# Graph attention in four layers: the softmax weights transposed in 32x32 blocks by VectorE and ScalarE, layer 3's products issued from a list

## The chip, the core and the metric

The kernel runs on one core of a Trainium2 chip. A core has a matrix engine (TensorE, PE in the profile; its weight loads are PEld), a vector engine (VectorE, DVE), a scalar engine (ScalarE, ACT), GpSimd (POOL) and SyncE (SP), which mainly starts DMA transfers. Each engine works through its own list of instructions in order; semaphores make one wait for another. TensorE reads SBUF and writes PSUM[...]. The metric is the time of one execution on the device in microseconds, the median of several runs.

## What is computed

The input x has 128 graphs of 64 nodes with 512 features, fp32, so 8192 rows; adj has a 64x64 mask for each graph. Four layers run one after the other, each with a residual:

```
h = relu(layernorm(x))
x = x + layer(h, adj)
```

Layers 0 and 2 are attention with 4 heads of 64, layer 1 is attention with 8 heads and a layernorm of its own. In these the weights of a head are

```
sim  = q @ k.T * scale             # 64 x 64 in a graph and head
attn = softmax(where(mask, sim, very negative))
out  = attn @ v                    # then @ Wo + bo
```

Layer 3 forms m = h @ map_w.T, then q and k from m, and sem = h @ gcn_map_w.T. For each of 8 heads the cosine of m's rows is compared with 0.1, the 0/1 result multiplies the softmax of q and k, each row is divided by its sum + 1, and the weights are applied to sem; relu, residual, output. The softmax runs along a row of a 64x64 block, which lies along the free dimension, while the sum over neighbours needs that index on the partitions. So each block of weights has to be transposed between the two. That is what the change is about.

## The kernel before

The rows are worked in 16 steps of 512 (8 graphs, that is four blocks b of 128 rows with two graphs g each), layer by layer. A step of a layer goes through layer norm (scales, normalize), transposes of h (transposes), the projections, the scores and softmax (front), and the weighted sum with the output projection (attention; in layer 3 last).

The projections are large products. Each runs as a scheme of seven half-sized products in place of eight (winograd, lines around 640, with product at L581 for the matmuls): a full one is seven products of eight 128x256 passes. Sums of the operands are made by POOL (L362) or VectorE (L359). The results leave PSUM through ScalarE (L598, L602, L618) and VectorE (L611, L622); three PSUM banks mA, mB and mC are used in turn, and a product can begin in a bank only after ScalarE has read the last one out of it.

The scores of a unit fill two PSUM banks S, 128x1024 values (L870): 16 blocks of 64x64. Layers 0 and 2 have one unit in a step, layers 1 and 3 two, so 96 units in all. On each unit come: a mask (VectorE, L881), the row maximum (L887), subtraction into an SBUF tile E (L889), exp on ScalarE (L892), row sums (L899), a reciprocal (L903) and the division by POOL (L905). In layer 3 the cosine scores (L870 again, of the m tiles), a comparison (L1135), a product (L1144) and more sums come in between.

transposed (L906 to L920) then turns E: eight 128x128 transposes by TensorE against an identity, into two PSUM tiles ptp, each brought to the SBUF tile pt by ScalarE (L919). The weighted sum (L1035, in layer 3 L1175) multiplies pt with v. A 128x128 transpose takes two graphs and two heads at once, so scores puts the two graphs of a block side by side on the free dimension, and two heads one above the other. The mask in SBUF therefore is 128 wide for each block of rows, and holds both graphs on all partitions.

The order of all work is set while the program is built. Every piece of work is a Python generator, a stream, which yields an engine, an assumed duration and a latency before each instruction, or an event to wait for. Order.run takes the stream that can start earliest by these durations, ties by priority (a smaller number first), and emits its instruction. An eviction of PSUM (priority 0) goes ahead of other work on ScalarE and VectorE that would still run when it becomes due (urgent). On the chip the order is fixed; if a stream is late there, what stands behind it on the engine is late too.

Buffers: E has three, pt and S one each, PSUM tiles ptp share two buffers with the transposes of h. Weights go through a ring of four buffers (r_w) in the order of units: q3 takes the buffer of layer 2's w_qk, k3 that of w_vo, which layer 2's last output projection still reads.

The projections of layer 3 were emitted step by step: map, sem, q, k for steps 0 to 13, and for the last two steps map, map, q and k, q and k, sem, sem. norms makes the lengths of m's rows: squares by ScalarE (L809), four small matmuls (mmn, L814), a way through DRAM to spread them over the partitions, and a product by POOL (L850). It waits for the end of layer 2's stores (x_done).

Of the kernel before, what the change touches and what calls it, by code (L numbers as in the profile page):

```python
# [16 lines left out]
N = 64  # L17
# [7 lines left out]
NEG_L3 = -1e10 * 8  # L25

# [201 lines left out]
def gnn_stack(ctx: ExitStack, tc: tile.TileContext, a: dict, out: bass.AP):  # L228
# [26 lines left out]
    r_e = ring("e", 3, [P, 16, N])  # L255
    r_c = ring("c", 1, [P, 2, 512], U8)
    r_pt = ring("pt", 1, [P, 2, 4, P])
    r_adj = ring("adj", 2, [P, TB, P], U8)
    r_n0 = ring("n0", 2, [P, TB, P], U8)
# [74 lines left out]
    for key, _ in units:  # L334
        w_ready[key], w_sums[key] = od.event(), od.event()
    wv_sums = {0: od.event(), 2: od.event()}
# [184 lines left out]
    def transposes(steps):  # L521

        for l, s in steps:
# [20 lines left out]
            if (l, s) == (3, 1):  # L544
                yield x_done[2, NG - 1]
# [149 lines left out]
    st, p_ready, s_ready, p_used, late = {}, {}, {}, {}, []  # L695

    def projections(steps):
        for l, s in steps:
# [37 lines left out]
            else:  # L736
                m_part = yield from map_part(s, z, BT)
                if s < NG - 2:
                    yield from sem_part(s, z, BT, m_part[1])
                    yield from qk_part(s, z, *m_part)  # L740
                else:

                    late.append((s, z, BT, m_part))
        for s, z, BT, m_part in late:
            yield from qk_part(s, z, *m_part)
        for s, z, BT, m_part in late:
            yield from sem_part(s, z, BT, m_part[1])

    def map_part(s, z, BT):
        yield w_ready["map3"]  # L750
        mT, z["m_done"] = yield from r_m.new("mT")
        m_ready = yield from unit(W["map3"], (*BT, w_sums["map3"]), False, Out(quarters(mT), map_b))
        m_sums, z["n_ready"], m_used = od.event(), od.event(), od.event()
        od.spawn(when([m_ready], w_done["map3"] if s == NG - 1 else None), 0)
        od.spawn(sums_after(m_ready, quarters(mT), z, m_sums, s == NG - 1), 1)
        od.spawn(norms(mT, s, m_ready, z["n_ready"], m_used), 3)
        return mT, m_ready, m_sums, m_used

    def qk_part(s, z, mT, m_ready, m_sums, m_used):
        es = []  # L760
        for n in "qk":
            yield w_ready[f"{n}3"]
            yield m_sums
            o, z[f"{n}_done"] = yield from r_qk.new(f"{n}T3")
            es.append((yield from unit(
                W[f"{n}3"], (quarters(mT), z["T"], w_sums[f"{n}3"]), False,
                Out(quarters(o), q_b if n == "q" else k_b))))
            z[n] = o
        z["n"] = mT
        od.spawn(when(es, s_ready[3, s], m_used, z["T_done"]), 0)  # L770

    def sem_part(s, z, BT, m_ready):

        yield w_ready["sem3"]
        V, z["v_done"] = yield from r_v.new("S2")

        def sv(i, k):
            return V[:, 2 * k:2 * k + 2, i * H:(i + 1) * H]
        used = yield from unit(W["sem3"], (*BT, w_sums["sem3"]), True, Out(sv))
        od.spawn(when([m_ready, used], t_done[3, s], h_done[3, s]), 0)  # L780
        rows = od.event()
        od.spawn(add_rows(V, used, rows), 0)
        z["v"] = V
        od.spawn(when([rows], p_ready[3, s]), 0)
# [15 lines left out]

    def norms(mT, s, m_ready, ready, used):

        yield m_ready
        yield x_done[2, NG - 1]
# [12 lines left out]
        yield dve(0.69)  # L817
        nc.vector.tensor_copy(ss, p_)
        pe_.set()
# [4 lines left out]
        se.set()  # L824

# [10 lines left out]
        nr = []  # L836
        for c in range(NC):
# [17 lines left out]
    def scores(lT, rT, npair, blocks):  # L855
        S, e = yield from r_sc.new("sc")
        nch = npair // 2
        nb = len(blocks)
        for b, t in enumerate(blocks):
            for ch in range(nch):  # L860
                j = ch * nb + b
                yield quads(0.235)
                for g in range(2):
                    k = slice(t * P + g * N, t * P + (g + 1) * N)
                    col = slice((2 * j + g) * N, (2 * j + g + 1) * N)
                    for a_ in range(2):
                        for par in range(2):
                            c = 2 * ch + (a_ ^ par)
                            r = slice(par * N, (par + 1) * N)
                            nc.tensor.matmul(S[a_ * N:(a_ + 1) * N, par, col],  # L870
                                             lT[r, c, k], rT[r, c, k], start=True, stop=True)
# [35 lines left out]
    def transposed(E, e):  # L907

        Ev = E.rearrange("p (i g) k -> p i (g k)", g=2)
        o, oe = yield from r_pt.new("pt")  # L910
        for par in range(2):
            pt, pe_ = yield from r_tr.new("ptp")
            for j in range(4):
                yield pe(0.115)
                nc.tensor.transpose(pt[:, j, :], Ev[:, par * 4 + j, :], ident)  # L915
            if par:
                e.set()
            yield act(0.6)
            nc.scalar.copy(o[:, par], pt)  # L919
            pe_.set()  # L920
        return o, oe

    def masks(l, s):

        adj, ae = yield from r_adj.new()
        n = TB * P
        yield load(3.5)
        nc.sync.dma_start(adj.rearrange("p b k -> p (b k)"), a["adj"][:, s * n:(s + 1) * n])
        av = adj.rearrange("p b (g k) -> p (b g) k", k=N)
        n0, ne = yield from r_n0.new()  # L930
        nv = n0.rearrange("p b (g k) -> p (b g) k", k=N)
        if l == 3:
            nz = small.tile([P, TB * 2], U8, tag="nz", name="nz", bufs=1)
# [324 lines left out]
```

## Time and profile before

The kernel takes 2898.45 us, the median of 3 runs (2894.9 to 2902.67). In the profiled execution the granted clock of TensorE was 0.994 on average. Busy time in windows that lie inside one layer each:

| window, us | layer | PE busy | VectorE | ScalarE | POOL |
|---|---|---|---|---|---|
| 30 to 540 | 0 | 509.75 | 356.90 | 267.56 | 338.25 |
| 545 to 1440 | 1 | 893.89 | 500.90 | 400.05 | 379.67 |
| 1450 to 1930 | 2 | 479.59 | 306.41 | 239.31 | 305.49 |
| 1945 to 2750 | 3 | 805.00 | 462.00 | 336.81 | 411.76 |
| 2750 to 2790 | 3 | 34.41 | 22.53 | 12.80 | 10.05 |

In such a table the busy time of each engine is held against the length of the window. The groups of the profile give a line of the code, the engine, what is written and read, the shape and the count, then busy time and mean time of one, then the idle time ahead of them and what ended it. The instructions that the change removes are the L915 group on PE (768 matmuls with a median of 273 ns each by the records, which overlap) and the L919 group on ScalarE (192 of 588 ns).

### The profile page before, as it was taken

To read this page: it belongs to the slowest core of one execution; us is meant where nothing else is said; L and a number is where in the kernel's file an instruction comes from. 1 tells how busy PE (TensorE), PEld (TensorE's weight loads), DVE (VectorE), ACT (ScalarE), POOL (GpSimd) and SP (SyncE) were. 2 spreads that over 40 slices of the span, in tenths; PEclk is the share of its full clock that TensorE was granted. 3 is DMA by queue.
4 is the path that set the end of the run, shared out by engine and by line. 5 is a ranking of instruction groups with operands and counts; after the bars stand their busy time and mean duration, and the time that the engine had idled before them with its cause. 6 is when DMAs were issued, how large, how long until landed. Compare 5 with 4: busy or idle time off the path is not lost.

```text
span 2895.9 us, 64997 instructions
## 1 busy us (share of the span) xinstructions
PE 2853.7 (99%) x27944; PEld 2483.3 (86%) x27944; DVE 1730.6 (60%) x2628; ACT 1315.1 (45%) x2265; POOL 1514.1 (52%) x1158
## 2 busy tenths in 40 slices
PE   8999999999999999999999999999999999999998
PEld 7898988888888888888888898978888888888877
DVE  7766666754565556454557666636665556655446
ACT  4555555444444444433445455544444444344332
POOL 6756566544343433344647656665445544455443
PEclk9999999999999999999999999999999999999999
DMA  4324233221112111112322323323222322232221
GB/s 154 133 90 135 90 121 103 79 74 61 45 46 74 61 46 61 60 61 78 119 90 94 131 90 134 105 88 91 62 63 81 90 69 61 61 83 67 64 62 45
DMA packets 160433, 240.70 MB, mean 83 GB/s; under 512 B 15761, under 2 KB 69009, under 8 KB 160145
## 3 DMA queue, kind: packets, MB, share of 16 engines
q1 hardware_dynamic: 145632, 222.08, 24.4%
q10 hardware_dynamic: 14512, 14.47, 1.5%
q8 instruction: 219, 3.59, 0.5%
q14 instruction: 70, 0.57, 0.1%
HBM read 168.87 MB, written 67.63 MB: 82 GB/s over the span
## 4 chain that ended last, share of the span: by engine, by line
PE 96%; DVE 1%; DMA 1%; POOL 1%; issue 0%; ACT 0%; SPq 0%; DVEq 0%; ACTq 0%; POOLq 0%
PE mA L581 46%; PE mC L581 23%; PE mB L581 11%; PE sc L870 5%; PE ptr L535 3%; PE ptp L915 3%; PE po L1035 2%; PE po L1175 1%; PE ptr L512 1%; PE mmn L814 1%; POOL E L905 0%; DMA w_o<-in_Wo 0%; DMA out<-xres 0%; DMA xin<-in_x 0%; DVE sm L899 0%
## 5 line engine op out<-in xcount | busy, mean ns | idle before, releaser
L981 POOL TENSOR_TENSOR xres<-xres,u 128x512 f32<-128x512 f32 x192 | 247.1, 1294 | 274.7 <-ACT u L976 271.2
L439 DVE BATCH_NORM_STATS2 st<-xin 128x6 f32<-128x512 f32 x320 | 216.8, 678 | 156.0 <-DMA xin<-x 118.1
L960 POOL TENSOR_TENSOR xres<-xres,u 128x512 f32<-128x512 f32 x192 | 267.7, 1415 | 36.0 <-DMA xres<-x 21.8
L446 POOL TENSOR_TENSOR rs<-rs,mhalf 128x2 f32<-128x2 f32 x160 | 115.6, 726 | 276.5 <-DVE rs L444 265.8
L455 ACT ACTIVATE xin<-xin,rs 128x512 f32<-128x512 f32 x320 | 248.9, 810 | 18.4 <-DVE rs L448 17.7
L362 POOL TENSOR_TENSOR t<-hT 128x512 f32<-128x512 f32 x126 | 161.5, 1282 | 114.4 <-ACT hT L517 80.4
L598 ACT COPY v<-mA 128x256 f32<-128x256 f32 (+1 forms) x192 | 91.9, 478 | 282.9 <-PE mA L581 274.4
L581 PE MATMUL mA<-w_vo,t 128*128 128x128 f32 (+1 forms) x1152 | 205.3, 310 | 0.0
L581 PE MATMUL mA<-t,w_q 128*128 128x256 f32 x744 | 190.5, 383 | 0.0
L581 PE MATMUL mA<-t,w_qk 128*128 128x256 f32 x768 | 187.4, 380 | 1.4 <-DVE t L359 1.4
L362 POOL TENSOR_TENSOR t<-hT,t 128x512 f32<-128x512 f32 x126 | 162.7, 1291 | 40.9 <-ACT hT L517 37.3
L905 POOL TENSOR_TENSOR E<-E,sm 128x1024 f32<-128x1024 f32 x64 | 123.4, 1929 | 112.0 <-DVE sm L903 81.4
L581 PEld LDWEIGHTS mA<-w_vo,t 128*128 128x128 f32 x1152 | 168.4, 191 | 12.5 <-ACT u L976 1.1
L899 DVE TENSOR_REDUCE sm<-E 128x16 f32<-128x1024 f32 x128 | 155.3, 1213 | 35.6 <-ACT E L892 34.9
L581 PE MATMUL mA<-t,w_k 128*128 128x256 f32 x744 | 175.9, 379 | 0.0
L581 PEld LDWEIGHTS mA<-t,w_qk 128*128 128x128 f32 x768 | 143.2, 190 | 19.7 <-DVE t L359 1.6
L919 ACT COPY pt<-ptp 128x512 f32<-128x512 f32 x192 | 112.7, 588 | 102.6 <-PE ptp L915 101.4
L581 PEld LDWEIGHTS mA<-t,w_k 128*128 128x128 f32 x744 | 141.2, 190 | 19.1
L976 ACT COPY u<-mA 128x512 f32<-128x512 f32 x144 | 84.4, 586 | 146.7 <-PE mA L581 143.9
L581 PEld LDWEIGHTS mA<-t,w_q 128*128 128x128 f32 x744 | 132.4, 190 | 15.3
L540 ACT COPY hT<-ptr 128x512 f32<-128x512 f32 x192 | 112.7, 588 | 55.0 <-PE ptr L535 55.0
L798 POOL TENSOR_TENSOR v<-v,gcn_row 128x512 f32<-128x512 f32 x64 | 79.2, 1268 | 106.1 <-ACT v L598 106.1
(217 smaller groups left out, 6966.0 us busy)
## 6 DMA issues: line engine op xcount, KB each, us to landing
x<-xres SPq DMA_DIRECT2D x96, 512.0 KB
xin<-x SPq DMA_DIRECT2D x96, 512.0 KB
xres<-x SPq DMA_DIRECT2D x64, 512.0 KB
xres<-in_x SPq DMA_DIRECT2D x32, 512.0 KB
u<-rs SPq DMA_DIRECT2D x128, 128.0 KB
xres<-x SPq DMA_DIRECT2D x64, 256.0 KB
out<-xres SPq DMA_DIRECT2D x64, 256.0 KB
xin<-in_x SPq DMA_DIRECT2D x30, 512.0 KB
```

The costliest lines, as they stand in the source:

```text
L362: nc.gpsimd.tensor_tensor(o, i0, i1, ALU.subtract)
L439: nc.vector.bn_stats(st, v[:, t, :])
L446: nc.gpsimd.tensor_tensor(rs[:, 0, :], rs[:, 1, :], mhalf[:, :2], ALU.pow)
L455: nc.scalar.activation(v[:, t, :], v[:, t, :], func, bias=rs[:, 2, t:t + 1], scale=rs[:, 0, t:t + 1])
L540: nc.scalar.copy(h[:, :, b * P:(b + 1) * P], pt)
L581: nc.tensor.matmul(o, l, r, start=(first and m == 0 and k == 0), stop=(k == KC - 1), skip_group_check=True)
L870: nc.tensor.matmul(S[a_ * N:(a_ + 1) * N, par, col], lT[r, c, k], rT[r, c, k], start=True, stop=True)
L899: nc.vector.tensor_reduce(o, E, AX.X, ALU.add)
L905: nc.gpsimd.tensor_mul(E, E, sm[:, :, None].to_broadcast([P, 16, N]))
L919: nc.scalar.copy(o[:, par], pt)
L960: nc.gpsimd.tensor_add(xr[:, t, :], xr[:, t, :], bo[l])
L981: nc.gpsimd.tensor_add(v, v, both(u))
```

## The change

The transposes leave TensorE. VectorE can transpose each 32x32 block of a tile in place of its own; for a 64x64 block that leaves the two off-diagonal blocks in the wrong places. So ScalarE first copies E to a tile F in eight pieces, each of 32 partitions and 16 x 32 elements, which moves blocks between partitions; then one VectorE instruction transposes all 32x32 blocks of F into pt. E is free after the copies, so it has two buffers; F has one. As blocks are now 64 wide, scores keeps a graph on its own 64 partitions, and masks and cosine masks are half as wide; the host sends half of the mask.

```diff
     def transposed(E, e):
 
-        Ev = E.rearrange("p (i g) k -> p i (g k)", g=2)
+        F, fe = yield from r_f.new("F")
+        for g in range(2):
+            for i in range(2):
+                for k in range(2):
+                    yield act(0.587)
+                    nc.scalar.copy(F[g * N + 32 * k:g * N + 32 * (k + 1), :, 32 * i:32 * (i + 1)],
+                                   E[g * N + 32 * i:g * N + 32 * (i + 1), :, 32 * k:32 * (k + 1)])
+        e.set()
         o, oe = yield from r_pt.new("pt")
-        for par in range(2):
-            pt, pe_ = yield from r_tr.new("ptp")
-            for j in range(4):
-                yield pe(0.115)
-                nc.tensor.transpose(pt[:, j, :], Ev[:, par * 4 + j, :], ident)
-            if par:
-                e.set()
-            yield act(0.6)
-            nc.scalar.copy(o[:, par], pt)
-            pe_.set()
+        yield ("dve", 1.2, 1.0)
+        nc.vector.transpose(o, F)
+        fe.set()
         return o, oe
...
-    r_e = ring("e", 3, [P, 16, N])
+    r_e = ring("e", 2, [P, 16, N])
+    r_f = ring("f", 1, [P, 16, N])
```

The transposes of a unit are no longer called by attention; a stream of their own, turns, takes the units in order and sets pt_ready.

```diff
         for u, blocks in enumerate(units):
-            yield z["e_ready", u]
-            pt, pte = yield from transposed(*z["e", u])
+            yield z["pt_ready", u]
+            pt, pte = z["pt", u]
...
+    def turns(steps):
+
+        for l, s in steps:
+            yield p_used[l, s]
+            z = st[l, s]
+            for u in range(len(units_of(l)[1])):
+                yield z["e_ready", u]
+                z["pt", u] = yield from transposed(*z["e", u])
+                z["pt_ready", u].set()
```

The second part concerns layer 3. Its projections come from a written list; the first two steps are interleaved, so that other products stand between q and k of step 0. What step 1 waits for becomes earlier: o_taken is set when layer 2's last output sums have their buffer.

```diff
+        order = [("map", 0), ("sem", 0), ("q", 0), ("map", 1), ("k", 0), ("sem", 1), ("q", 1), ("k", 1)]
+        for s in range(2, NG - 2):
+            order += [(n, s) for n in ("map", "sem", "q", "k")]
+        order += [(n, s) for n in ("map", "qk", "sem") for s in (NG - 2, NG - 1)]
...
             if (l, s) == (3, 1):
-                yield x_done[2, NG - 1]
+                yield o_taken
...
     def norms(mT, s, m_ready, ready, used):
 
         yield m_ready
-        yield x_done[2, NG - 1]
+        if s == 0:
+            yield o_done
+        elif s < NG - 1:
+            yield lengths[s - 1]
```

Smaller edits of order: residuals of neighbouring steps take their buffers in turn, an output projection waits for the one before it, the copy of the lengths out of PSUM gets priority 0, and the loads of lengths for step 14 wait until step 15 has sent its squares. Outside the 768 transposes, TensorE has the same matmuls as before, in the same shapes.

## The prediction, made before the changed kernel was run

> **What bounds the kernel now.** I read the engines' busy shares first, then the chain that ended last, then TensorE's own waits, then the timeline around the instructions that the change removes.
>
> ```profile
> PE 2853.7 (99%) x27944; PEld 2483.3 (86%) x27944; DVE 1730.6 (60%) x2628; ACT 1315.1 (45%) x2265; POOL 1514.1 (52%) x1158
> ...
> PE 96%; DVE 1%; DMA 1%; POOL 1%; issue 0%; ACT 0%; SPq 0%; DVEq 0%; ACTq 0%; POOLq 0%
> ```
>
> TensorE (PE) is busy 99% of the span and is 96% of the chain. A busy PE need not be one at its peak, so I looked at what it waits for:
>
> ```profile
> PE ptr L535 <- ACT xin L455: 11.2, 1, 11.2
> PE mA L581 <- DMA w_k<-in_k: 4.5, 1, 4.5
> PE mC L581 <- DVE xres L611: 3.7, 1, 3.7
> PE ptp L915 <- POOL E L905: 2.2, 2, 1.9
> ```
>
> The columns are total, times, longest. All of PE's waits come to some 33 us, a third of it the start. Three sit at borders of layers or near the end; in the steady part of a layer PE waits for nobody (from 545 to 1440 us, layer 1, it is busy for 893.89 of 895). So the time is the sum of PE's starts, and an edit is worth what it takes out of that row. What one transpose takes is in the timeline of layer 1:
>
> ```profile
> 601.31 1.03 PE L581 MATMUL mA<-t,w_q 128*128 128x256 f32 x4
> ...
> 602.18 0.60 PE L915 MATMUL ptp<-ident,E 128*128 128x128 f32 x4
> ...
> 602.62 1.89 PE L581 MATMUL mC<-t,w_q 128*128 128x256 f32 x8
> ```
>
> From the start of the four transposes to the start of the next product are 0.44 us, so 0.110 us each, not the 0.273 us of one record: records overlap. Four product passes before them take 602.18 - 601.31 = 0.87 us, 0.217 each, the same as inside a run of products (eight in 1.73 us elsewhere), so switching between the two costs nothing extra.
>
> [...] The record here is 273 ns, but the interval of 110 ns is what counts. [...] The squares of the norms, SBUF to SBUF with 512 elements, agree (619 ns each, started 520 ns apart: four took 2.19 us).
>
> **The change part by part.**
>
> 1. Transposes leave PE. 96 softmax units (16 steps x (1 + 2 + 1 + 2) units) x 8 = 768, the count of the L915 row. 768 x 0.110 = **84.5 us off the path**. The chain's own share, 3% of 2896 rounded, agrees. The products have the same count and shapes, as do scores and weighted sums (32 small matmuls per pair of banks[...]): only which head lies where changes. I take zero for these.
>
> 2. ScalarE. Out: 192 evictions of 588 ns, 112.7 us. In: 96 x 8 = 768 copies of 32 partitions x 512 elements. ScalarE's groups have these rows (busy, mean ns, idle before); the last is the nearest, from SBUF to SBUF:
>
> ```profile
> L455 ACT ACTIVATE xin<-xin,rs 128x512 f32<-128x512 f32 x320 | 248.9, 810 | 18.4 <-DVE rs L448 17.7 <-issue 0.7
> ...
> L919 ACT COPY pt<-ptp 128x512 f32<-128x512 f32 x192 | 112.7, 588 | 102.6 <-PE ptp L915 101.4
> ...
> L809 ACT ACTIVATE u<-m 128x512 f32<-128x512 f32 x64 | 36.5, 621 | 1.0 <-issue 1.0
> ```
>
> I expect 0.52 us apart and 0.61 each; bounds 0.50 and 0.81 (the row of L455, with two pointer operands, should the strided 32-partition form be slow). 768 x 0.52 = 399, so ScalarE goes from 1315 to about 1602, 57% of the new span; upper bound 1315 - 113 + 622 = 1824, 65%. Layer 0 is the densest: 268 us of 510 now (52%), 16 x (8 x 0.52 - 1.18) = 48 more, against 510 - 14 = 496: 64%. Off the path as long as PSUM evictions aren't held up. One copy is a separate instruction, and in the new order evictions stand between the copies (typically one to four copies, an eviction, one to four copies), so an eviction finds at most a few copies ahead of it that were planned there.
>
> 3. VectorE. In: 96 transposes of 128x1024. No row shows one; the nearest is a pass over 1024 fp32 elements:
>
> ```profile
> L899 DVE TENSOR_REDUCE sm<-E 128x16 f32<-128x1024 f32 x128 | 155.3, 1213 | 35.6 <-ACT E L892 34.9
> ```
>
> I take its 1.21 us[...]. 96 x 1.21 = 116. Out: masks on half the columns, as a block's mask is now 64 wide: 64 passes of 0.5 to 1.8 us (28.3 + 16.2 + 12.6 us) and 16 small ones, saving perhaps 28, half of them. 1731 + 116 - 28 = 1819, 65%. Hidden.
>
> 4. The wait that this adds. A unit's way from E normalized to transposed was two groups on PE and two evictions, about 3.4 us in the window above (first transpose at 602.18, second eviction 605.03 + 0.59, with a product between). Now it is 8 x 0.52 + 1.2, with gaps about 5.5 us. Behind an F copy that waits for E on ScalarE stand evictions, and for these PE waits. The old kernel's PE stood in the same place (L915 behind POOL's E): it waited 2.2 us in 96 units, so E comes when the order expects it. E's buffers go from 3 to 2, but a new unit comes only every 28 to 30 us in layers 1 and 3 (895 us for 16 steps of two units in layer 1, 61 us a step in layer 3) and every 30 to 32 in layers 2 and 0, and E is now free after the copies, before the weighted sum. I cost it at zero in the steady part, with up to 0.3 us a unit as the risk.
>
> 5. Layer 3's list. Before, k of step 0 stood behind q of step 0 and waited for w_k: 4.5 us in the wait rows. w_k lands in the buffer of layer 2's w_vo, so only after layer 2's last product. The list puts the map of step 1 there, seven products of 1.73 us, 12 us, enough to hide a 4.3 us load. **-4.5 us.** This needs the hT of step 1 earlier: its transposes now wait for the last layer-2 sums only, and stand inside the map of step 1.
>
> 6. Near the end, PE waits of 2.2 us (ptp for E) go with the transposes. The stall around 2758 to 2768 us stays: the map of step 15 needs the buffer of step 13's map, which its cosine scores release.
>
> 7. The tail. In the order of before, the last cosine scores start 12 us before the last product ends; in the new order 0.9 us before it (two matmuls of two passes), since E has two buffers and layer 3's E waits for the copies of the step before. Before, the last product ends at 2877 and the span 19 us later. Now from that end: VectorE's neighbour passes 4.5, POOL's row additions and division to about +9, copies 4.2, transpose 1.4, weighted sum 1.1, then 6.4 us from the last VectorE pass to the end as before (2889.54 to 2895.9): 22.1. **+3.5 us.**
>
> Sum: 2898.5 - 84.5 - 4.5 - 2.2 + 3.5 = **2811 us**.
>
> **The rivals.**
> - ScalarE jitter. Copies sit ahead of evictions when E is late, and a product waits. For it: ScalarE at 64% in layer 0, and strictly in order. Against: only 2.2 us of waits for E now, and 1 us or more of slack between two products on one bank (another product of 1.73 us lies between). At 0.3 us a unit, 96 x 0.3 = 29: 2840. At one whole copy, 0.6, 2869.
> - Slower than before. If the small copies take twice what the row says (1.2 us) and the transposes 2.4, a unit takes 12 us on ScalarE and VectorE, 6.5 more than planned, and everything in order behind it is late. If a quarter of it, 1.6 us, reaches PE in each unit, 96 x 1.6 = 154: 2965. [...]
> - More is gained. The borders fill too (3.7 us at 1442, 2.3 idle between 500 and 600, 5.6 idle between 2750 and 2790): 2811 - 11.6 = 2799. For it: the same list moves steps there. Against: only the border to layer 3 is named in the edit.
>
> **How the numbers follow.** The forecast's case has 0.70, ScalarE jitter 0.16, more gained 0.09, slower 0.05. The range reaches down past the third rival, to 2797, and up past the lower jitter case, 2846. Faster 0.94, same 0.02, slower 0.04.
>
> **What would show it.** PE's instructions fall by 768, and the L915 row is gone; the product rows keep their counts and means. Copies of F near 0.61 us each, the transpose near 1.21. ScalarE near 1600 us busy. The wait for w_k is gone. In PE's waits no row with a long total over many times behind ScalarE or VectorE; such a row (mA or mC behind ACT, tens of us over some 90 times) would be the jitter rival. A last product's end some 22 us before the span's end. I would be wrong if an F copy takes over 0.8 us, or if PE's busy share falls under 97%.

## The result, and the profile after

The changed kernel takes 2820.2 us, the median of 4 runs (2818.71 to 2823.6), beside 2897.81 us for the kernel before in runs of the same chip (2894.9 to 2902.67). The ratio is 0.9732, with a 95% interval of 0.9715 to 0.9749: 77.6 us less. The forecast was 2811, so some 9 us of the expected gain did not come.

The engines' busy shares of the profiled execution and, below them, its chain of waits by engine:

```profile
PE 2766.3 (98%) x27176; PEld 2398.8 (85%) x27176; DVE 1822.2 (65%) x2724; ACT 1679.4 (60%) x2841; POOL 1539.3 (55%) x1158
...
PE 90%; DVE 4%; POOL 3%; ACT 1%; issue 1%; DMA 1%; POOLq 0%; ACTq 0%; SPq 0%; DVEq 0%
```

PE has 27176 instructions in place of 27944, 768 fewer. Its busy time fell by 2853.7 - 2766.3 = 87.4 us. VectorE is where the forecast had it (1819 forecast, 1822 measured); ScalarE is 77 us above (1602, 1679). PE's part of the chain fell from 96% to 90%, and the others' parts grew: something now waits that did not before.

The two groups of instructions that are new (line, engine, operation, output and input, count, then busy time, mean ns of one, idle time ahead):

```profile
L946 ACT COPY F<-E 32x512 f32<-32x512 f32 x768 | 472.5, 615 | 53.7 <-POOL E L937 43.0
L951 DVE STREAM_TRANSPOSE pt<-F 128x1024 f32<-128x1024 f32 x96 | 118.6, 1235 | 50.5 <-ACT F L946 50.4
```

A copy takes 615 ns (forecast 0.61) and a transpose 1235 (forecast 1.21). Busy time counts overlapping records once, and 472.5 / 768 = 615: no overlap is left in it, though the forecast counted 0.52 us a copy.

PE's own waits, the largest (total us, times, longest):

```profile
PE ptr L539 <- ACT xin L459: 11.5, 1, 11.5
PE po L1214 <- DVE pt L951: 10.7, 2, 5.7
PE po L1069 <- DVE E L921: 3.9, 6, 1.1
PE mB L585 <- DVE xres L615: 3.8, 3, 1.3
PE mC L585 <- DVE xres L615: 3.6, 3, 1.7
PE sc L902 <- DVE E L921: 3.2, 2, 1.6
```

The first is the start, as before. The row for w_k is gone. The second is the end of the kernel, where two weighted sums wait for their transposes. The others are new or longer. They have few occurrences, and the releaser is VectorE, not ScalarE; the rows of banks mA, mB and mC behind ScalarE, not shown here, come to 5.1 us in six waits. (A product bank is read out by VectorE too, as the rows with xres show, and not by ScalarE alone, as was said of the kernel before.) The windows tell where they lie (in each row the window, its length, then busy time and count of PE, PEld, VectorE, ScalarE and POOL, the granted clock, DMA's share and GB/s):

```profile
30.00:535.00 505.00, 496.07 (x4822) 441.28 (x4821) 372.95 (x574) 328.07 (x550) 343.42 (x269) 1.00 0.34 114
545.00:1400.00 855.00, 854.85 (x7721) 742.20 (x7720) 526.86 (x815) 517.02 (x795) 369.77 (x291) 1.00 0.18 63
1425.00:1840.00 415.00, 408.26 (x4009) 365.00 (x4007) 290.17 (x443) 259.77 (x447) 276.86 (x215) 1.00 0.32 110
1900.00:2680.00 780.00, 778.36 (x8325) 657.71 (x8325) 482.91 (x667) 435.86 (x809) 414.17 (x280) 1.00 0.26 73
```

PE is idle for 8.9 of 505 us in layer 0 and 6.7 of 415 in layer 2, but for 0.15 of 855 in layer 1 and 1.6 of 780 in layer 3. In the kernel before, the window from 30 to 535 us had PE busy for 504.75. Layers 0 and 2 are those where VectorE is fullest: 373 / 505 = 74% and 70%, against 62% in layers 1 and 3. ScalarE is at 65% and 63% there, and 60% and 56% in the other two.

From the starts and ends of PE's instructions in the trace I made a ledger of PE's idle time by layer (layers divided at the first product with a layer's first weights, layer 0 counted from 30 us on; the tail runs from the end of the last product to the end of the span):

| us | layer 0 | layer 1 | layer 2 | layer 3 | length of the tail |
|---|---|---|---|---|---|
| before | 0.3 | 2.9 | 4.1 | 10.6 | 18.9 |
| after | 8.9 | 1.1 | 6.7 | 6.6 | 24.0 |

The changes come to +8.6 - 1.8 + 2.6 - 4.0 + 5.1 = +10.5. With the 84.5 us of the transposes that is -74.0; the two profiled executions lie 2821.8 - 2895.9 = -74.1 apart. So the ledger closes, and the question is what the +8.6, +2.6 and +5.1 are. That it closes to 0.1 us is partly chance: PE's busy time fell by 87.4 us, not by 84.5. The ledger counts idle time alone; time in which PE works at a lower clock is not in it. In the kernel before the trace shows half the full clock granted for 6.8 us from 1445 us and for 3.4 us from 1937 us, at the two long waits at borders of layers (gaps between PE's starts of 4.3 us from 1442 and 5.0 us from 1932), and in all such stretches product passes start 426 ns apart in place of 216; after the change no border has such a stretch. In all stretches of this kind PE is busy for 22 us before and for 10 after.

### The profile page after: what moved, and what is told of

It is laid out like the page before. It is cut to its first block, busy times and chain, and to the rows that moved or that the text cites. A ratio compares the mean times of both kernels' runs of the same rounds, so it can differ in the third digit from the quotient of the medians.

```text
span 2821.8 us, 64271 instructions
## 1 busy us (share of the span) xinstructions
PE 2766.3 (98%) x27176; PEld 2398.8 (85%) x27176; DVE 1822.2 (65%) x2724; ACT 1679.4 (60%) x2841; POOL 1539.3 (55%) x1158
## 4 chain that ended last, share of the span: by engine, by line
PE 90%; DVE 4%; POOL 3%; ACT 1%; issue 1%; DMA 1%; POOLq 0%; ACTq 0%; SPq 0%; DVEq 0%
PE mA L585 44%; PE mC L585 22%; PE mB L585 11%; PE sc L902 5%; PE ptr L539 3%; PE po L1069 2%; PE po L1214 1%; PE ptr L516 1%; ACT F L946 1%; POOL t L366 1%; POOL xres L996 1%; PE mmn L844 1%; DVE t L363 1%; POOL E L937 1%; POOL xres L1017 1%
## 5 line engine op out<-in xcount | busy, mean ns | idle before, releaser
L946 ACT COPY F<-E 32x512 f32<-32x512 f32 x768 | 472.5, 615 | 53.7 <-POOL E L937 43.0
L1017 POOL TENSOR_TENSOR xres<-xres,u 128x512 f32<-128x512 f32 x192 | 249.3, 1305 | 207.1 <-ACT u L1012 162.5
L996 POOL TENSOR_TENSOR xres<-xres,u 128x512 f32<-128x512 f32 x192 | 257.0, 1360 | 88.3 <-DMA xres<-x 41.1
L366 POOL TENSOR_TENSOR t<-hT 128x512 f32<-128x512 f32 x126 | 170.6, 1354 | 144.0 <-ACT hT L544 82.8
L450 POOL TENSOR_TENSOR rs<-rs,mhalf 128x2 f32<-128x2 f32 x160 | 122.9, 770 | 170.4 <-DVE rs L448 128.8
L366 POOL TENSOR_TENSOR t<-hT,t 128x512 f32<-128x512 f32 x126 | 169.7, 1347 | 35.4 <-ACT hT L521 32.2
L931 DVE TENSOR_REDUCE sm<-E 128x16 f32<-128x1024 f32 x128 | 155.2, 1212 | 42.3 <-ACT E L924 41.7
L585 PE MATMUL mA<-t,w_q 128*128 128x256 f32 x744 | 181.2, 380 | 0.9 <-ACT qT L602 0.9
L951 DVE STREAM_TRANSPOSE pt<-F 128x1024 f32<-128x1024 f32 x96 | 118.6, 1235 | 50.5 <-ACT F L946 50.4
L1012 ACT COPY u<-mA 128x512 f32<-128x512 f32 x144 | 84.4, 586 | 107.9 <-PE mA L585 102.2
L937 POOL TENSOR_TENSOR E<-E,f 128x1024 f32<-128x1024 f32 x32 | 63.8, 1994 | 129.9 <-DVE nz L965 65.0
```

The costliest lines, as they stand in the source:

```text
L366: nc.gpsimd.tensor_tensor(o, i0, i1, ALU.subtract)
L450: nc.gpsimd.tensor_tensor(rs[:, 0, :], rs[:, 1, :], mhalf[:, :2], ALU.pow)
L585: nc.tensor.matmul(o, l, r, start=(first and m == 0 and k == 0), stop=(k == KC - 1), skip_group_check=True)
L931: nc.vector.tensor_reduce(o, E, AX.X, ALU.add)
L937: nc.gpsimd.tensor_mul(E, E, sm[:, :, None].to_broadcast([P, 16, N]))
L946: nc.scalar.copy(F[g * N + 32 * k:g * N + 32 * (k + 1), :, 32 * i:32 * (i + 1)], E[g * N + 32 * i:g * N + 32 * (i + 1), :, 32 * k:32 * (k ...
```

## The experiments

**The slope of the transposes on PE.** The kernel before, with each transpose issued twice:

```diff
-                yield pe(0.115)
-                nc.tensor.transpose(pt[:, j, :], Ev[:, par * 4 + j, :], ident)
+                for _ in range(2):
+                    yield pe(0.115)
+                    nc.tensor.transpose(pt[:, j, :], Ev[:, par * 4 + j, :], ident)
```

> The kernel before with each of the 768 transposes issued twice into the same place, the order made for it. If the span is the sum of TensorE's starts, 768 x 0.110 = 84.5 us are added: 2895.4 + 84.5 = 2980. If something beside TensorE took up part of the gain, the slope is smaller: under 2960.

2979.39 us, ratio 1.0289 [1.0276, 1.0303], beside 2894.95: **+84.4 us** for 768 more transposes, 0.110 us each. The order was made anew for them. The group in this trace:

```profile
L916 PE MATMUL ptp<-ident,E 128*128 128x128 f32 x1536 | 199.1, 273 | 1.0 <-POOL E L905 1.0
```

A record is 273 ns long, as before, while the transposes of a group start 0.109 us apart (median). The two profiled executions lie 82.9 us apart, 79.3 of it PE's busy time, so the agreement is to within a few us and not to a tenth. Step 1 of the prediction holds, and with it the reading that the interval between starts counts, not the 273 ns of a record.

**The two parts apart.** First the transposes alone: the softmax part of the change, with layer 3's products in the order of before (`yield x_done[2, NG - 1]` again in place of `o_taken`, the loops with `late` in place of the list, and `norms` as before).

> The kernel before with the new transposes alone (copies by ScalarE, VectorE's transpose, the turns stream, narrow masks, and the two edits that keep residuals and output projections in their order), layer 3 emitted step by step as before. The sum of TensorE's starts says that this is nearly all: the changed kernel's 2820 plus the 4.5 us wait for w_k, so 2824 to 2826, with the wait back in TensorE's rows at the border of layer 3. If the list costs something of its own (rival), this is at or under 2820. TensorE's idle time inside layers 0 and 2, 8.9 and 6.7 us in the changed kernel, is there too if the transposes cause it.

2831.52 us, 0.9777 [0.9764, 0.9791], beside 2895.41: -63.9, and more than the 2824 to 2826 us that were expected. The list is worth 11.3 us on top of it by the two medians (13.7 when each kernel is held against the kernel before of its own round; 7.7 between the profiled executions), not 4.5. PE's waits of this run:

```profile
PE po L1183 <- DVE pt L920: 13.3, 3, 5.8
...
PE sc L871 <- DVE E L890: 8.8, 9, 1.6
```

The second row is what the list removes: scores wait for the last unit's subtraction nine times for 8.8 us, against two times for 3.2 us in the changed kernel. There is no row for w_k here either, though the list is absent; so the list is not needed to take that wait away. (This kernel keeps the two edits that hold residuals and output projections in order, so it may be these or the transposes.) The idle time in layers 0 and 2 is the same as in the changed kernel (8.9 and 6.6).

Then the list alone: the kernel before with the list and the smaller edits of order, transposes on TensorE, three buffers of E.

> The kernel before with layer 3's list and all edits of order, transposes on TensorE as before. List hides the load of w_k: 2897.8 - 4.5 = 2893, to 2890 if the border of layer 2 gains too. Layers 0 and 2 show under 1 us of TensorE idle time, as before. Rival: residuals in turn and the output projection waiting for the one before are what makes TensorE wait in layers 0 and 2; then this kernel shows some 15 us of idle there and takes 2905 or more.

2889.53 us, 0.998 [0.9971, 0.9989]: -5.9. PE's idle time in layers 0 and 2 is 0.3 and 4.1, as before. So the new waits there come with the transposes, not with the edits of order alone.

**More load on ScalarE.** Each copy of F issued twice, to the same place:

```diff
-                    yield act(0.587)
-                    nc.scalar.copy(F[g * N + 32 * k:g * N + 32 * (k + 1), :, 32 * i:32 * (i + 1)],
-                                   E[g * N + 32 * i:g * N + 32 * (i + 1), :, 32 * k:32 * (k + 1)])
+                    for _ in range(2):
+                        yield act(0.587)
+                        nc.scalar.copy(F[g * N + 32 * k:g * N + 32 * (k + 1), :, 32 * i:32 * (i + 1)],
+                                       E[g * N + 32 * i:g * N + 32 * (i + 1), :, 32 * k:32 * (k + 1)])
```

> The changed kernel with each copy of F made twice, and the order made for it: 768 more ScalarE instructions, 480 us more ScalarE work. If copies lie beside TensorE, layers 1 and 3 don't move, the tail grows by two units' copies (10 us) and layers 0 and 2, where ScalarE goes from 65% to over 80%, by some more: 2835 to 2855. If each unit's copies were on the path, 96 x 5 us would show: about 3300. If ScalarE's load had nothing to do with the waits in layers 0 and 2, these stay at 15 us: 2830.

3059.54 us, 1.0569 [1.0553, 1.0585], so +239 over the changed kernel. The expectation failed by far: copies are not hidden at any load. The second copy of each pair waits for the first one's semaphore and starts 32 ns after its end. ScalarE's busy time goes from 1679 to 2143, 70% of the new span, and PE's waits are now of a kind that the changed kernel does not have:

```profile
PE mA L585 <- ACT u L1013: 52.3, 15, 4.7
PE po L1070 <- DVE pt L952: 47.0, 18, 8.0
PE po L1215 <- DVE E L921: 43.7, 14, 9.6
```

The first row is of the kind that the jitter rival described, a bank that ScalarE has not read out yet: in 13 of its 15 waits the four ScalarE instructions ahead of the eviction are copies of F. It comes as a few long waits of up to 4.7 us, not as some 90 short ones. The waits are not all of the loss. With the same 27176 matmuls, PE's busy time grows as well (the first line of the page, whose counterpart for the changed kernel stands above):

```profile
PE 2845.2 (93%) x27176; PEld 2445.9 (80%) x27176; DVE 1812.3 (59%) x2724; ACT 2142.8 (70%) x3609; POOL 1530.5 (50%) x1158
```

The mean granted clock is 0.966 here and 0.995 in the changed kernel. This trace has 31 stretches with half the full clock, 210 us together, against two of 30 us; inside them neighbouring product passes start 0.427 us apart, elsewhere 0.216. So of the 242 us between the two profiled executions 163 are idle time and 79 are PE's busy time. PE is busy for 140 us inside such stretches, and for 10 in the changed kernel; at half the rate that is worth some 65 of the 79 us, an estimate from these figures.

Here a unit's way is longer as well, so the next run takes the load alone: eight copies of 32x512 between places of an unused tile for each unit, in a stream that nothing waits for. The tile is bf16 and the copies are contiguous, but one takes 616 ns in the median, where a copy of F takes 615 in the changed kernel.

```diff
+    def more_copies():
+        for g in range(2):
+            for i in range(2):
+                for k in range(2):
+                    yield act(0.587)
+                    nc.scalar.copy(junk[g * N + 32 * k:g * N + 32 * (k + 1)],
+                                   junk[g * N + 32 * i:g * N + 32 * (i + 1)])
...
+                od.spawn(more_copies(), 3)
```

> The changed kernel with the same extra ScalarE load as in e4, eight more copies of 32x512 for each unit, the order made for them, but into a tile that nobody reads, from a stream of their own: they lengthen ScalarE's work and not a unit's way from E to pt. e4 took 3060. If its loss was the longer way of a unit (waits for pt and for PSUM behind it), this is far less: 2825 to 2860. If it was ScalarE's load and the evictions behind copies, this is as slow as e4: 3000 or more.

2955.03 us, 1.0202 [1.0189, 1.0215]: +135. It lies between the two expectations. PE's waits, the first two rows:

```profile
PE mA L587 <- ACT u L1014: 38.6, 15, 5.2
PE po L1071 <- DVE pt L953: 21.8, 8, 6.1
```

From the first copy of F to the end of the transpose a unit takes 8.8 us here (median of 96), as in the changed kernel, and 16.5 with the doubled copies. So of the 239 us a little more than half comes with load alone. The rest is put down to the longer way of a unit, by subtraction; the orders of the two kernels differ too. Of the 133 us between this profiled execution and the changed kernel's, 44 are PE's busy time, with a mean granted clock of 0.978 and PE busy for 88 us at half the full clock. Layer 0 idles 36.5 us here and 76.9 in the run before it.

**The duration in the plan.** The planner assumes 0.587 us for a copy; the trace shows neighbours 0.626 apart. With the truer number:

```diff
-                    yield act(0.587)
+                    yield act(0.63)
```

> The changed kernel with one number changed: the order is made with 0.63 us for a copy of F in place of 0.587, as copies on the chip start 0.626 us apart. If the waits in layers 0 and 2 (some 15 us) come from an order made for copies that are too short, most of it goes: 2806 to 2812. If the engines beside TensorE are too full there whatever the order, nothing changes: 2817 to 2823, with 12 us or more idle in layers 0 and 2.

2838.49 us, 0.9802 [0.9789, 0.9816]: 18 us worse. Both expectations missed. No instruction was added; only the order differs. Layer 0 idles 7.5 (1.4 better), layer 2 13.0 (6.3 worse), layer 3 8.9, and the tail is 30.0 us long in place of 24.0. A planned duration nearer to the measured one thus did not give a better order, and one such number moves this kernel by 18 us.

**The tail.** The last step's units transposed by TensorE as 64x64 blocks, everything else as changed:

```diff
-                z["pt", u] = yield from transposed(*z["e", u])
+                how = by_tensor if (l, s) == (3, NG - 1) else transposed
+                z["pt", u] = yield from how(*z["e", u])
```

> The changed kernel, but the two units of the very last step (layer 3, step 15) are transposed by TensorE, 32 matmuls of 64x64 against the identity, and brought out by two ScalarE copies each. In the changed kernel the last weighted sums wait 5.0 and 5.75 us for pt while TensorE has nothing left. If copies and VectorE's transpose (5.0 + 1.25 us) set the tail's end, the last unit's way falls to about 2.5 us: 2820 - 4 = 2816, the tail from the last product 24.0 to about 20. Rival: row additions by POOL and the residual's load are as late anyway: 2818 to 2821.

2818.69 us, 0.9737 [0.9724, 0.9749], beside 2894.95: the rival's range. The tail is 21.6 us in place of 24.0; the profiled executions differ by 6.3, but the medians by 1.5, and the two intervals of the ratio overlap. The way through ScalarE and VectorE at the very end is thus worth some 2.4 us by these two traces, and no gain in time is shown.

**Three buffers of E, or two.** The kernel before with `ring("e", 2, ...)` in place of 3:

> The kernel before with two buffers in place of three for the exponentials E; nothing is left out. The change as a whole went from three such buffers to two. Theory A: a buffer of E is free again long before the next unit but one needs it, so the number of buffers has no part in what the change fell short by: 2893 to 2900 us, and no more than 1 us of idle time on TensorE in the layers 0 and 2. Theory B: part of the waits that appeared in the layers 0 and 2 of the changed kernel comes from the third buffer that is gone: 2900 to 2912 us, with 5 us or more of idle time on TensorE in those layers.

2901.64 us, 1.0018 [1.0008, 1.0027], beside 2896.46: +5.2. Each theory has half of it. PE's idle time in layers 0 and 2 is 0.3 and 4.0, as in the kernel before (the 4 us at the border of layer 2 were left out of the expectation), so the buffer by itself has no part in the waits there. But the last product ends at 2872 us in place of 2877, and the tail is 27.0 us in place of 18.9. This is step 7's argument on its own: with two buffers the last scores are made later. Here the last cosine scores start 8 us after the end of the last product; in the kernel before, 12 us ahead of it. In the order of before, the loss of the third buffer lengthens the tail by 8 us. Of these 5 are work of PE that moved from ahead of the last product to behind it, for PE's idle time in the four layers is the same.

**VectorE in place of ScalarE.** Half of the copies (the upper 64 partitions) moved to VectorE, with the transpose of F as before. ScalarE's busy time falls by 241 us, to 1439:

```diff
+        od.spawn(moved(E, F, 1, dve(0.45), nc.vector.tensor_copy, other), 1)
+        yield from moved(E, F, 0, act(0.587), nc.scalar.copy, od.event())
+        yield other
```

> The changed kernel with the four copies of the second graph made by VectorE, beside the four of the first by ScalarE, the order made for 0.45 us a VectorE copy. A unit's way gets 2.5 us shorter, ScalarE's load falls by 236 us, VectorE's grows by 96 x 4 x 0.35 to 0.61 = 134 to 234. If the length of the way makes the waits in layers 0 and 2 and the tail, these shrink: 2806 to 2814. Rival: the waits follow from how full the order is, VectorE's included, or change with any number in the plan as in e3: 2815 to 2840.

2937.7 us (2935.4 to 2962.3), 1.0172 [1.0141, 1.0203]: slower than before. The trace's answer for the tile F on VectorE (count, then the duration in ns: minimum, median, maximum), and below it the same group as the profile gives it, with the mean:

```profile
L944 DVE COPY F<-E x384: 417/423/2106, 45.9 to 2925.1; 32x512 f32<-32x512 f32 x192
```

```profile
L944 DVE COPY F<-E 32x512 f32<-32x512 f32 x384 | 318.4, 829 | 21.8 <-POOL E L937 15.3
```

The median is 423 ns but the mean 829. Sorted by whether POOL was at work, the 137 copies with POOL idle take 421 ns, and the 247 that overlap an instruction of POOL 1055 on average. Of these, 149 are held up: they take 1470 on average, and each ends 280 to 290 ns after an instruction of POOL does; the other 98 take some 420, as with POOL idle. What holds a copy back is not shown; but the 96 transposes of F by VectorE in the same run all take 1185 to 1246 ns. The order had been made for 0.45 us a copy. So the same division was tried with transposes in place of VectorE's copies. One can read a strip of 32 partitions and write to another, at 705 ns for 32x512 in the run below, so that it moves and transposes in one; the upper 64 partitions go this way from E to pt:

```diff
+                yield dve(0.62)
+                nc.vector.transpose(o[N + 32 * k:N + 32 * (k + 1), :, 32 * i:32 * (i + 1)],
+                                    E[N + 32 * i:N + 32 * (i + 1), :, 32 * k:32 * (k + 1)])
```

> As e7, the first graph's blocks copied by ScalarE, the second's moved by VectorE; but VectorE doesn't copy: four of its 32-partition transposes take the blocks from E straight into pt, turned and moved at once. In e7 a VectorE copy took 0.42 us where POOL did nothing and up to 2.1 us where it worked, while VectorE's transposes of 128 partitions took 1.24 us either way. If that holding back is what made e7 slow (2938), these take some 0.6 us each whatever POOL does, and the kernel comes to 2820 to 2840. If VectorE is simply too full, or the order for two engines bad, it stays near 2938.

2837.59 us, 0.9798 [0.9785, 0.9811], 100 us better than with the copies at the same division of partitions and much the same busy time of VectorE (2077 us, and 2084 there). The planned durations differ too (0.63 for ScalarE's copies in place of 0.587, and 0.62 for VectorE's part in place of 0.45), so not all of the 100 us need be the holding back. The trace's answer for these transposes, in the same columns:

```profile
L943 DVE STREAM_TRANSPOSE pt<-E x384: 702/705/711, 45.6 to 2828.1; 32x512 f32<-32x512 f32 x192
```

All 384 lie within 702 to 711 ns, 84 of them with POOL idle and 300 with POOL at work. Compared with the changed kernel the last product ends at about the same time (2797.0 and 2797.8 us); nearly all of the loss is in a tail of 40.2 us. There the last cosine scores start 12 us after the end of the last product (in the changed kernel 2 us ahead of it), and each unit's way then has five transposes on VectorE.

**Why ScalarE's copies don't overlap.** In the changed kernel full-tile ScalarE instructions start some 100 ns before the record of the last one ends, and F copies 12 ns after. Each copy reads from, or writes to, another start partition than the last one. So each copy was split into two halves of 8 blocks, between the same partitions:

```diff
-                    yield act(0.587)
-                    nc.scalar.copy(F[g * N + 32 * k:g * N + 32 * (k + 1), :, 32 * i:32 * (i + 1)],
-                                   E[g * N + 32 * i:g * N + 32 * (i + 1), :, 32 * k:32 * (k + 1)])
+                    for b in (slice(0, 8), slice(8, 16)):
+                        yield act(0.41)
+                        nc.scalar.copy(
+                            F[g * N + 32 * k:g * N + 32 * (k + 1), b, 32 * i:32 * (i + 1)],
+                            E[g * N + 32 * i:g * N + 32 * (i + 1), b, 32 * k:32 * (k + 1)])
```

> The changed kernel with each of ScalarE's copies that move a quarter of the exponentials to other partitions issued as two copies of 8 blocks each, between the same partitions, 1536 in place of 768; nothing is left out. In the changed kernel one copy records 615 ns and two neighbours start 626 ns apart, though ScalarE's full-tile operations start some 100 ns sooner than the last one's record ends. Theory A: the loss of the overlap comes with the change of the start partition from copy to copy. Then the second half of a copy, between the same partitions as the first, starts about 0.31 us after it, where halves record about 0.41 us, and ScalarE's busy time stays near 1700 to 1760 us. Theory B: it comes with any copy that does not start at partition 0. Then the second half starts 0.41 us or more after the first, ScalarE is held for about 0.83 us a quarter, and with 160 us more to do the kernel takes 2860 to 2960 us, as the other runs with more work on ScalarE did.

2826.48 us (one run). The timeline of the last unit in the changed kernel and in this one, ScalarE's lines alone (start, length in us of the whole run of instructions, their count at the end):

```profile
2806.96 5.00 ACT L946 COPY F<-E 32x512 f32<-32x512 f32 x8 [2.73 <-POOL E L937]
```

```profile
2809.10 5.74 ACT L947 COPY F<-E 32x256 f32<-32x256 f32 x16 [1.37 <-DVE pt L953]
```

Eight copies take 5.00 us, sixteen halves only 5.74, though a half records 400 ns. In all of the trace the second half starts 310 ns after the first (92 ns before the first's record ends, 598 cases), and the next copy, between other partitions, 410 ns after (12 ns behind the end, 516 cases). That is theory A: **the overlap is lost at a change of the start partition**. The changed kernel's trace agrees. Of its 480 neighbouring F copies none overlap, and in 292 of these pairs only the partition written to changes. Where a unit's first copy, between the first 32 partitions, follows a full tile, which starts there too, it starts some 100 ns before the end in 42 of 48 cases. It is not the only way to lose the overlap: the doubled copies above, between the same partitions, wait for a semaphore and start 32 ns after the end. With the split copies PE's idle time in layers 0 and 2 is 5.1 and 0.4 us, less than in the changed kernel, with ScalarE at 1758 us; the loss is in layer 1 (6.5), layer 3 (9.5) and the tail (30.8).

**Putting two together.** The last step on TensorE as above, and a planned duration of 0.65:

> The kernel of e5 with the order made for 0.65 us a copy of F. e3 (0.63) showed that a small change in this number moves the time by 18 us, the wrong way. If what an order costs is set by how its pieces happen to fall and not by how true the number is, another number can as well be better: with fewer planned gaps 2806 to 2814. If a price above the true 0.626 is harmful as such, this is slower than e3: 2838 or more.

2815.1 us, 0.9725 [0.9712, 0.9738], beside 2896.44, the lowest of all kernels here, though its interval overlaps the changed kernel's. Layer 0 idles 7.3 us, layer 2 4.1, layer 3 4.9. A planned 0.63 had made it worse, 0.65 with another tail does not; I take this as the order's luck, not as a rule for that number.

## Why the prediction was right, and where it was short

The mechanism held: PE bounds the kernel, the change takes 84.5 us off it, and most of the work that replaces it is hidden. By the prediction's steps:

1. **Transposes leave PE, -84.5.** Right: +84.4 when they were doubled, though 79 to 83 by the profiled executions, and products run at the same rate in both traces (0.216 us between the starts of neighbouring passes).
2. **ScalarE's copies, 0.61 each and 0.52 apart.** The duration was right (0.615), the interval wrong: 0.626. The row that it came from, the squares of the norms, writes full tiles, where neighbours do overlap (619 ns each, started 520 apart); the split copies show that a change of partitions ends this (12 ns from the end of one to the start of the next). The copies come to 472.5 us in place of the 399 forecast, 73 of the 77 us by which ScalarE's busy time is above it. Nor did a 64x64 transpose need ScalarE to move blocks, as the change has it: in the run with half of them turned by VectorE, its transposes wrote blocks to other partitions themselves, at 705 ns each.
3. **VectorE.** Right in both terms: 1235 ns against 1.21 us, and 1822 us in all against 1819.
4. **The added wait, costed at zero in the steady part.** This is the step that failed, by its size. A unit's way was counted at 5.5 us and takes 8.8 in the median, from the first copy of F to the end of the transpose: as other ScalarE instructions stand between the copies, these alone stretch over 6.9 us, where eight in a row take 5.0. The prediction named up to 0.3 us a unit as a risk; layers 1 and 3 show none, layers 0 and 2 together 15.6 us in 32 units. Of these 4.4 were there before, of which 3.7 was the wait at the border of layer 2 that the third rival hoped to fill; it is gone. So new are 11.2 us by the ledger's totals, or 14.9 if the border is counted as a gain of its own. The transposes alone show the same idle time, the list alone no more than before, and two buffers of E in the kernel before no more either.
   The prediction looked for such waits behind ScalarE. In the window of layer 0 (30 to 535 us) PE's rows of waits behind VectorE come to 6.8 us, those behind ScalarE to 1.9. One of the longest leads to POOL. Lines of the timeline of the changed kernel from 184 to 194 us (start, length, engine, line, output and input, count, in brackets the idle time ahead and what ended it):

```profile
187.47 1.90 POOL L937 TENSOR_TENSOR E<-E,sm 128x1024 f32<-128x1024 f32 x1 [2.17 <-DVE sm L935]
...
189.48 0.71 POOL L450 TENSOR_TENSOR rs<-rs,mhalf 128x2 f32<-128x2 f32 x1
...
190.16 2.49 POOL L996 TENSOR_TENSOR xres<-xres,u 128x512 f32<-128x512 f32 x2
...
192.68 0.69 DVE L615 TENSOR_TENSOR xres<-mB,xres 128x512 f32<-128x512 f32 x1 [1.16 <-POOL xres L996]
...
193.43 0.92 PE L585 MATMUL mB<-hT,w_qk 128*128 128x256 f32 x3 [1.27 <-DVE xres L615]
```

   Read it from below: a product waits 1.27 us until VectorE has read bank mB out; that eviction waits 1.16 us for POOL's additions to the residual; these stand behind a small layer-norm step and the division of a unit's weights, and POOL goes from one to the next with 0.1 us of idle time at most. The division itself had waited 2.17 us for its reciprocals. No copy of F is in this chain. The same stall, 1.28 us, stands at 427 us in the same form. Neither the length of a unit's way nor ScalarE's load explains the 11.2 us by itself. With the split copies ScalarE is busier by 78 us and the way is longer (14.0 us in layer 0 and 11.4 in layer 2, medians, against 8.6 and 8.8), yet the two layers idle 5.5 us in place of 15.6. With half of the transposes moved by VectorE the way is shorter (6.6 and 5.9), yet layer 0 idles 10.3 in place of 8.9 (layer 2 2.6 in place of 6.7). Layers 1 and 3 have the same way as layers 0 and 2 and few waits. What is left is how the order makes its pieces fall on engines that are fuller than before. That is argued and not shown: each of these kernels has an order of its own, and why this one waits where it does stays open.
5. **Layer 3's list, -4.5.** Mis-sized: -5.9 by itself, -11.3 on top of the transposes. The reason given did not carry it on top of the transposes: there the w_k wait is absent without the list too, and what the list removes there is mostly waits of scores for the softmax's subtraction, nine of 8.8 us in all against two of 3.2.
6. **The late stall stays.** It does, at 2688 to 2696 us; the two longest waits of scores (1.6 and 1.3 us) lie there.
7. **The tail, 22.1, +3.5.** Measured 24.0, +5.1. The eight copies were counted at 4.2 us and take 5.0; the line of the last unit above shows it, and the transpose follows at 2812.00, 0.04 us after their end. The last weighted sum was counted at 1.1 us and takes 2.0, in a stretch where half the full clock was granted:

```profile
2813.39 1.99 PE L1214 MATMUL po<-v,pt 64*64 64x64 f32 x64 [5.75 <-DVE pt L951]
```

   That two buffers of E set the late scores is confirmed by the run that removed one.

In sum, with the transposes taken at their forecast -84.5, the steps that mattered came as new waits in layers 0 and 2 of +11.2 (0), layers 1 and 3 of -5.8 (-6.7, for the list and the waits that went with the transposes), tail +5.1 (+3.5). That the miss was only 9 us is partly luck: the same kernel with one planned number changed takes 2838, 27 us above the forecast. The rival of ScalarE jitter is refuted for this kernel as it stands, since no row of mA or mC behind ScalarE is long, but it is what happens as soon as ScalarE gets more to do: the doubled copies brought such a row. The slower rival asked for copies of 1.2 us and transposes of 2.4; the doubled copies alone, at some 1.27 us a pair, gave 3059 where it had 2965, so its size was too small.

"Hidden at 60% busy" was too strong a sentence. The engine's mean load said that there was room, and yet 8 more copies a unit cost 135 us even with nothing waiting for them, and of the 133 us between the profiled executions 44 are not idle time but slower matmuls, at a granted clock of 0.978 on average in place of 0.995. ScalarE works in order and also empties the product banks (u<-mA alone is 144 copies of 586 ns in the changed kernel); here it hid work only in the places that the order found for it.

## What to carry to other kernels

Take from the bound engine by the interval between starts; in this kernel that part came in full (84.4 us measured for 84.5). For what is put on other engines, use the interval of an instruction that also changes partitions (0.626 us here, where full tiles had shown 0.52), and don't cost it at zero because the engine is at 60%: look at the layer where it and its neighbours are fullest. In this one kernel the waits there came to a third to half of a microsecond a unit. Count the work that the order sets between the pieces too, and look at the granted clock as well as at idle time: with the doubled copies 79 of the 242 us were longer busy time of PE. Where an order is planned, a single assumed duration can move the result by 18 us, so differences of this size between two variants say little on the edit itself unless the ledger of idle time tells where they lie.

## What the runs showed of the hardware

- Neighbouring ScalarE instructions overlapped by 92 ns (halves of copies, 598 cases) to some 100 ns (full tiles) between the same partitions. Where the start partition changes, be it only the one written to, none of the 480 neighbouring F copies of the changed kernel overlapped (12 ns between them); nor did the doubled copies, where the second waits for the first by a semaphore (32 ns).
- With half of the copies moved, VectorE's 32x512 copy from SBUF to SBUF takes 421 ns with POOL idle, 1055 on average and up to 2106 when POOL is at work; its transpose of the same size, in the run with half turned, takes 702 to 711 in every case. In the changed kernel the reductions over E (1212 ns on average) and the 128x512 additions from PSUM to qT, kT, qk and xres (689) take the same with POOL idle and at work.
- VectorE's transpose can write its blocks to other partitions than it reads, at 705 ns for 32x512; in place it takes 1235 for 128x1024. So ScalarE's copies are not needed to move blocks. What stands against it here is VectorE's own load: eight such transposes a unit would be 96 x 8 x 0.705 = 541 us in place of 119, an estimate from these two figures that no run tried.
- Where the trace shows half the full clock granted to TensorE, product passes start 427 ns apart in place of 216 (with the doubled copies; 426 and 216 in the kernel before). With the doubled copies PE's busy time was 79 us longer at the same number of matmuls, some 65 of it by this, as estimated above.
